# A graph layer's kernel: the order of the first loads, and the order of work behind the last gather

## The chip, the cores and the metric

The kernel runs on one core of a Trainium2 chip. A core has a matrix engine (TensorE, PE in the profile; PEld is its loading of weights), a vector engine (VectorE, DVE), a scalar engine (ScalarE, ACT), a general engine (GpSimd, POOL) and SyncE (SP), which here only issues transfers. SP and ACT have a hardware queue for transfers each; POOL issues gathers by indices through a queue that is written by software. All queues share 16 DMA engines. The metric is the time of one execution on the device, in microseconds; the time before is the median of three runs.

## The reference

A graph layer with 12,500 nodes of 96 channels and 412,500 edges, sorted by target node:

```
node_feat = mlp(x, W_node, ...)                   # relu, then normalized over all nodes
edge_feat = mlp(edge_attr_4, W_edge, ...)         # relu, then normalized over all edges
message   = mlp(concat(x[src], x[dst], edge_feat), W_msg, ...)   # relu, normalized over all edges
agg       = segment_sum(message, dst)
out       = layernorm(x + agg + node_feat)        # per node
```

Each `mlp` normalizes each channel with the mean and the variance over all its rows. The mean and mean square of the messages are therefore known only when the last edge has been worked on; scale and shift of the messages are applied behind the sum over edges.

## The kernel before, in words

*Tables.* x lies transposed in SBUF (`xp`, 96 partitions, 98 blocks of 128 nodes). `tables` (L153) multiplies each block by two thirds of W_msg and writes two tables to DRAM: `p_tab`, for the source node of an edge, and `q_tab`, for the target node. It goes by chunks of 14 blocks (`CH`), with two buffers of rows, and its writes alternate between the queues of SP and ACT.

*Gathers.* Edges go in tiles of 128, in groups of 4 tiles and blocks of 4 groups: 3,223 tiles, 806 groups, 202 blocks. For each tile POOL issues one gather (`gather`, L179) of the 128 source rows. The first 16 groups (`RAW` = 4 blocks, 64 gathers) are gathered from x itself, by a small piece of the indices (`src_raw`) that is loaded first of all, so that they need not wait for the tables; later (`convert`) TensorE multiplies them by the weights. All others come from `p_tab`, by `src`. The first 26 blocks (`SPILL`) are gathered while the statistics of nodes and edges are still being made, and written back to DRAM by SP; from then on gathers fill a ring of 26 groups (`RING`).

*Between.* `places`, `nodes` and `edge_norm` prepare the edges' places, the nodes' part and the edge statistics while the gathers go on.

*The main loop* (L624 to L663) works group by group in an order written out by hand for all five engines: `edges` and `prepare` compute the edge features, `linear` multiplies by weights and the window of `q_tab` rows, `message` (L514) adds the gathered rows. The message is clipped at zero and split into bf16 parts: `first_part` (L531, ACT), `second_part` (L566 on DVE, L567 on ACT), `third_part` (L572, DVE). `clipped` and `squared` (L537 and L541, ACT) make the squares for the statistic. `sums` (L584) multiplies by a 0/1 matrix, so that TensorE adds the edges of a node; `fold` (L590), `turn` (L594) and `add` (L607, L608) put a block's sums into `agg`.

*The end* (L665 to L708). The last block has two groups; `last` is the first of them, and `n - 1`, of three tiles, is the other. Each is worked on alone. POOL, which has no gathers left, adds up the squares (`collect`, L553 to L561). At the very end a product with a column of ones (L696) adds them over the partitions, and some small DVE and ACT instructions (L700 to L149) turn the sums into scale and shift. The stage `output` (L862) multiplies `shift` by a centering matrix (L868), then `agg` by a matrix `dm` (L879), and normalizes each node in 13 blocks.

*Unread products.* `unread` (L464) makes TensorE multiply 128x128 parts of `rel` by the identity, into a PSUM buffer that nobody reads: they keep the engine busy where it would have nothing to do. A call with n makes n products of 512 columns, two passes each.

The order of SP and POOL in the first part, and that of all engines in the main loop and the end, is that of the program's text; elsewhere a scheduler orders the instructions of an engine. Each engine executes its own in order, and so do the queues of transfers. What is in front of an instruction on its engine thus delays it.

Of the kernel before, what the change touches and what calls it, by code (L numbers as in the profile page):

```python
# [11 lines left out]
F32 = mybir.dt.float32  # L12
# [9 lines left out]
N, C, E, ED = 12500, 96, 412500, 4  # L22
EPS = 1e-5
P = 128
# [3 lines left out]
GT, GE, BG = 4, 512, 4  # L28
# [11 lines left out]
NB = -(-N // P)  # L40
NN = NB * P
NBK = 4
CH = 14
# [15 lines left out]
NW = WS * (BG - 1) + WN + 1  # L59
OW = NW * GT + WS * (BG - 1)  # L60
CL, CE = 2, 2
BUSY = 2
J = 8


# [12 lines left out]
def gnn(ctx, tc, t):  # L78
    nc = tc.nc
# [11 lines left out]
    src = const.tile([P, NTP], I32, name="src")  # L91
# [2 lines left out]
    ring = rpool.enter_context(tc.tile_pool(name="ring", bufs=RING // 2))  # L94
    xp = xpool.enter_context(tc.tile_pool(name="x", bufs=1)).tile([C, NN], F32, name="xp")
    nc.scalar.dma_start(w_msg, t["L0_gnn_W_msg"].rearrange("(s k) f -> k s f", k=C))
    for i in range(0, NB, CH):
        part = slice(i * P, (i + CH) * P)
        (nc.scalar if i // CH % 2 else nc.sync).dma_start(xp[:, part], t["xp"][:, part])
    nc.scalar.dma_start(src, t["src"])  # L100

    ident = const.tile([P, P], F32, name="ident")
    make_identity(nc, ident)
# [24 lines left out]
    rel = const.tile([P, NGP, GT], F32, name="rel")  # L128
# [224 lines left out]
    def fast(ring):  # L353
# [13 lines left out]
        with tc.manual_schedule(engines={ET.SP, ET.Pool}):  # L367
# [12 lines left out]
            n = 0  # L380
# [18 lines left out]
        with tc.tile_pool(name="fix", bufs=1) as fix, tc.tile_pool(name="msg", bufs=2) as work, \  # L399
# [62 lines left out]
                        got[b * BG + i] = back[:, i, :, :]  # L462

            def unread(n):  # L464
                busy = ps.tile([P, GE], F32, name="pa")
                for i in range(n):
                    nc.tensor.matmul(busy, ident, rel[:, i * P:(i + 1) * P, :].rearrange("p g t -> p (g t)"),
                                     start=True, stop=True)

            def convert(s):  # L470
# [62 lines left out]
            def clipped(k, m=2, n=GT):  # L533

                z, h = parts(k, m, n)
                sq = work.tile([P, 2, GT, C], F32, name="sq")
                nc.scalar.activation(sq[:, :m, :n, :], z, AF.Relu)  # L537
                return sq

            def squared(sq, m=2, n=GT):  # L540
                nc.scalar.activation(sq[:, :m, :n, :], sq[:, :m, :n, :], AF.Square)  # L541
                return sq, m, n
# [8 lines left out]
            def collect(x, n, r=P):  # L551

                plus = nc.gpsimd.tensor_add  # L553
                whole = n if r == P else n - 1
                if r < P:
                    plus(squares[:r], x[:r, whole * C:n * C], squares[:r])
                while whole > 1:
                    half = whole // 2
                    plus(x[:, :half * C], x[:, :half * C], x[:, (whole - half) * C:whole * C])
                    whole -= half  # L560
                plus(squares, x[:, :C], squares)  # L561

            def second_part(k, m=2, n=GT):

                z, h = parts(k, m, n)
                nc.vector.scalar_tensor_tensor(z, z, 0.0, h[0], op0=OP.max, op1=OP.subtract)  # L566
                nc.scalar.activation(h[1], z, AF.Copy)  # L567

            def third_part(k, m=2, n=GT):

                z, h = parts(k, m, n)
                nc.vector.tensor_tensor(h[2], z, h[1], op=OP.subtract)  # L572

            def sums(k):

                s, g = steps[k]
                n = min(GT, NT - g * GT)
                i = g % BG
                h, o = hb[s % HB][:, i, :, :, :], WS * (BG - 1 - i)
                if i == 0:  # L580
                    pas[s] = ps.tile([P, GE], F32, name="pa")
                for t in range(n):
                    r = min(P, E - (g * GT + t) * P)
                    nc.tensor.matmul(pas[s][:NW, :3 * (C + 1)], at[s % HB][:r, i, o + NW * t:o + NW * (t + 1)],  # L584
                                     h[:r, t, :, :].rearrange("p a c -> p (a c)"),
                                     start=i == 0 and t == 0, stop=t == n - 1 and (i == BG - 1 or g == NG - 1))
# [6 lines left out]
            def turn(s):  # L593
                nc.tensor.transpose(pas[s][:C + 1, GE - P:GE - P + NW], by_node.pop(s), ident[:NW, :NW])  # L594
# [16 lines left out]
            with tc.manual_schedule(engines={ET.SP, ET.Pool, ET.PE, ET.DVE, ET.Activation}):  # L611
                bad = nc.values_load(flag, min_val=0, max_val=1, skip_runtime_bounds_check_because="a comparison's result")
                load(0)
                fetch(0)
                load(1)
                fetch(1)
                for half in range(2):
                    edges(0, half)
                    prepare(0, half)
                edges(1, 0)  # L620
                for k in range(3):
                    linear(k)
                waiting, last = None, BG * (len(order) - 1)
                for k in range(last):  # L624
                    s, g = steps[k]
                    if g % BG == 0:
                        if s + 2 < len(order):
                            load(s + 2)
                            fetch(s + 2)
                    message(k)  # L630
                    j = k - LATER - BG - 1
                    if k % 2:
                        first_part(k - 1)
                        now = squared(clipped(k - 1))
                        if waiting:
                            moments(*waiting)
                        waiting = now
                        second_part(k - 1)
                    if j >= 0 and j % BG == 0:
                        fold(j // BG)  # L640
                    if j >= 2 and j % BG == 2:
                        add(j // BG, place(j // BG))
                    if k % 2:
                        third_part(k - 1)
                    if j >= 1 and j % BG == 1:
                        turn(j // BG)
                    if k >= LATER:
                        sums(k - LATER)
                    if g % BG != 3 and s + 1 < len(order):
                        if g % 2:  # L650
                            edges(s + 1, 1)
                        else:
                            prepare(s + 1, g % BG // 2)
                    if g % BG == 3:
                        if s + 1 < len(order) and order[s + 1] < RAW:
                            convert(s + 1)
                        if s + 2 < len(order):
                            edges(s + 2, 0)
                    if k + 3 < n:
                        linear(k + 3)  # L660
                    if g >= SPILL:
                        got[ahead] = ahead_of(ahead)
                        ahead += 1  # L663

                s, g = len(order) - 1, steps[last][1]  # L665
                m, r = NT - (g + 1) * GT, E - (NT - 1) * P
                collect(waiting[0].rearrange("p g t c -> p (g t c)"), 2 * GT)
                message(last)
                first_part(last, 1, GT)
                sq = clipped(last, 1, GT)  # L670
                turn(s - 2)
                add(s - 2, place(s - 2))
                sums(last - 2)
                sums(last - 1)
                unread(1)
                second_part(last, 1, GT)
                message(n - 1)
                first_part(n - 1, 1, m)
                squared(sq, 1, GT)
                collect(sq[:, 0, :, :].rearrange("p t c -> p (t c)"), GT)  # L680
                third_part(last, 1, GT)
                sums(last)
                fold(s - 1)
                at_end = place(s - 1), place(s)
                sq = clipped(n - 1, 1, m)
                second_part(n - 1, 1, m)
                turn(s - 1)
                squared(sq, 1, m)
                collect(sq[:, 0, :, :].rearrange("p t c -> p (t c)"), m, r)
                add(s - 1, at_end[0])  # L690
                third_part(n - 1, 1, m)
                sums(n - 1)
                square_sum = ps.tile([P, 2, GE], F32, name="pr", bufs=1)[:C, 0, :1]
                fold(s)
                turn(s)
                nc.tensor.matmul(square_sum, squares, ones, start=True, stop=True)  # L696
                unread(BUSY)
                mean_square = fix.tile([C, 1], F32, name="mean_square")
                add(s, at_end[1])
                nc.vector.tensor_scalar(mean_square, square_sum, 1.0 / E, None, op0=OP.mult)  # L700
                ahead_of(ahead)
                ahead_of(ahead + 1)
# [233 lines left out]
```

## Time and profile before

| | |
|---|---|
| time, median of 3 runs | 4107.81 us (4106.57 to 4109.8) |
| time of the profiled execution | 4088.25 us |
| its span | 4086.1 us |
| POOL busy | 3068.8 us, 75% of the span |
| PE, DVE, ACT busy | 3149.9, 2578.6, 2033.7 us |
| mean granted TensorE clock | 0.631 |
| moved by DMA | 274.06 MB, 67 GB/s in the mean |

How to read it: an engine's busy time is the sum of its instructions; between two gathers POOL also spends time on issue, which isn't counted as busy. The clock is a share of full speed, as granted to TensorE over a stretch. In a list of groups stands the line, the engine, the operation, what is written and read, how often, the total in us and the mean in ns, then the idle time ahead of them and what ended it. In the order of time a row has its start, its duration, engine, line, operation, and in brackets the idle time before it with what ended that. The chain is followed back from the last instruction, at each step to what released it.

### The profile page before, as it was taken

How to read it: one execution, taken by the hardware profiler on the slowest of the kernel's cores; microseconds unless marked ns; L12 is line 12 of the kernel's file. 1: busy time of each engine (PE TensorE's matmuls, PEld its weight loads, DVE VectorE, ACT ScalarE, POOL GpSimd, SP SyncE). 2: the span in 40 equal slices, each digit the busy share in tenths (PEclk: the TensorE clock that was granted, in tenths of full speed). 3: DMA queues.
4: the chain of work that ended last, by engine and by line, in shares of the span. 5: the costliest groups of instructions: out<-in, count | busy, mean ns of one | idle time of the engine just before them, and what ended most of it. 6: DMA issues, size and time to landing. Idle time of an engine off the chain costs nothing.

```text
span 4086.1 us, 42638 instructions
## 1 busy us (share of the span) xinstructions
PE 3149.9 (77%) x13544; PEld 2305.1 (56%) x13544; DVE 2578.6 (63%) x4036; ACT 2033.7 (50%) x2422; POOL 3068.8 (75%) x3252
## 2 busy tenths in 40 slices
PE   4699958888887777777777777777777777767876
PEld 3456636666665555555555555555555555555555
DVE  2599985666776655665566556655666556656666
ACT  1388845555555544454445444544444444544444
POOL 7777777777777777777777777777777777777776
PEclk7655556666666666666666666666666666666667
DMA  8555532222222122212212222122212221222123
GB/s 229 176 120 116 114 82 55 54 55 55 56 55 51 50 53 54 54 46 54 52 48 54 52 55 53 46 53 54 54 46 54 54 54 46 54 52 55 46 76 96
DMA packets 194110, 274.06 MB, mean 67 GB/s; under 512 B 121987, under 2 KB 122372, under 8 KB 192870
## 3 DMA queue, kind: packets, MB, share of 16 engines
q0 software_dynamic: 103136, 158.62, 16.3%
q1 hardware_dynamic: 77300, 103.96, 9.2%
q10 hardware_dynamic: 13440, 8.65, 0.8%
q8 instruction: 111, 1.82, 0.2%
q14 instruction: 123, 1.01, 0.1%
HBM read 227.56 MB, written 43.43 MB: 66 GB/s over the span
## 4 chain that ended last, share of the span: by engine, by line
POOL 46%; issue 18%; DMA 16%; PE 11%; DVE 8%; ACT 1%; DVEq 0%; POOLq 0%; ACTq 0%
POOL pg L179 46%; DMA pg<-p_tab,src 15%; PE z L505 5%; PE pa L584 3%; DVE sum_of L547 3%; PE pr L491 2%; DVE z L514 1%; DVE z L566 1%; ACT h L567 1%; DVE h L572 1%; DVE at L518 1%; PE pr L480 1%; DVE squares L549 0%; DMA pg<-in_x,src_raw 0%; PE pr L476 0%
## 5 line engine op out<-in xcount | busy, mean ns | idle before, releaser
L179 POOL DMA_INDIRECT pg<-p_tab,src x3159 | 2986.3, 945 | 966.1 <-issue 857.5
L505 PEld LDWEIGHTS z<-rhs,left 128*128 128x128 f32 x6446 | 1301.2, 297 | 1003.0 <-DVE h L572 887.9
L505 PE MATMUL z<-rhs,left 128*128 128x96 f32 x6446 | 1389.3, 388 | 566.7 <-DVE h L572 562.7
L531 ACT ACTIVATE h<-z 128x768 bf16<-128x768 f32 x404 | 329.9, 817 | 1352.3 <-DVE z L514 1346.9
L584 PE MATMUL pa<-h,at 128*80 128x291 bf16 x3223 | 850.4, 411 | 185.7 <-DVE at L518 181.8
L514 DVE TENSOR_TENSOR z<-z,pg 128x384 f32<-128x384 f32 x702 | 395.1, 563 | 773.1 <-DMA pg<-p_tab,src 741.2
L584 PEld LDWEIGHTS <-at 128*80 128x80 bf16 x3223 | 499.3, 168 | 299.2 <-DVE at L518 226.0
L547 DVE TENSOR_REDUCE sum_of<-sq 128x96 f32<-128x768 f32 x401 | 589.3, 1469 | 0.0
L499 ACT ACTIVATE left<-pr 127x1024 f32<-127x1024 f32 x403 | 410.8, 1019 | 307.2 <-PE pr L491 306.7
L572 DVE TENSOR_TENSOR h<-z,h 128x768 bf16<-128x768 f32 x404 | 386.8, 957 | 243.3 <-ACT h L567 242.8
L491 PE MATMUL pr<-ea,we 7*127 7x512 f32 x1404 | 498.8, 793 | 17.8 <-DMA ea<-rel_d 12.6
L566 DVE SCALAR_TENSOR_TENSOR z<-z,h 128x768 f32<-128x768 f32 x404 | 387.3, 959 | 30.4 <-ACT sq L537 30.2
L316 PE MATMUL pr<-ea,wide 10*128 10x512 f32 x1212 | 359.6, 1084 | 8.2 <-DMA ea<-in_ea 8.2
L322 DVE BATCH_NORM_STATS2 estats<-r 128x6 f32<-128x512 f32 x606 | 359.9, 676 | 7.8 <-ACT r L320 7.8
L567 ACT ACTIVATE h<-z 128x768 bf16<-128x768 f32 x404 | 328.9, 814 | 66.9 <-DVE z L566 66.9
L320 ACT ACTIVATE r<-pr 128x1024 f32<-128x1024 f32 x303 | 306.6, 1023 | 106.3 <-PE pr L316 62.8
L541 ACT ACTIVATE sq<-sq 128x768 f32<-128x768 f32 x404 | 339.7, 841 | 12.8
L537 ACT ACTIVATE sq<-z 128x768 f32<-128x768 f32 x404 | 323.2, 800 | 0.3 <-DVE h L572 0.3
L316 PEld LDWEIGHTS pr<-ea,wide 10*128 10x128 f32 x1212 | 239.6, 309 | 126.9 <-issue 65.7
L518 DVE TENSOR_TENSOR at<-rel,z 128x496 bf16<-128x496 f32 x202 | 135.6, 671 | 252.5 <-PE z L505 252.5
L491 PEld LDWEIGHTS pr<-ea,we 7*127 7x127 f32 x1404 | 133.3, 233 | 145.3 <-issue 127.0
L549 DVE TENSOR_TENSOR squares<-sum_of,squares 128x96 f32<-128x96 f32 x401 | 104.4, 260 | 13.8
(127 smaller groups left out, 1071.4 us busy)
## 6 DMA issues: line engine op xcount, KB each, us to landing
pg<-p_tab,src POOLq DMA_INDIRECT x3159
spill<-pg SPq DMA_DIRECT2D x52, 384.0 KB
pb<-spill SPq DMA_DIRECT2D x26, 768.0 KB
ea<-in_ea SPq DMA_DIRECT2D x75, 160.0 KB
rhs<-q_tab SPq DMA_DIRECT2D x202, 46.5 KB
ea<-in_ea SPq DMA_DIRECT2D x352, 20.0 KB
y_d<-y0s SPq DMA_DIRECT2D x12, 384.0 KB
pg<-y_d SPq DMA_DIRECT2D x12, 384.0 KB
```

Source lines behind the costliest of these rows:

```text
L179: nc.gpsimd.indirect_dma_start(out=pg[:, i, :], out_offset=None, in_=tab[:, :], in_offset=bass.IndirectOffsetOnAxis(ap=idx[:, k:k + 1], ax ...
L316: nc.tensor.matmul(pr[:, k % 2, :], wide[Q * i:Q * i + 2 * EK, :], ea[Q * i:Q * i + 2 * EK, b % J, :], start=True, stop=True)
L322: nc.vector.bn_stats(stats[:, (k - o) % NS, (k - o) // NS, :], r[:, 1 - o, :])
L491: nc.tensor.matmul(prs[s, half][:C + WN, i, :], we[o:o + EK + 2, :], block[s][o:o + EK + 2, :], start=True, stop=True)
L499: nc.scalar.activation(x[:C + WN, 2 * half:2 * half + n, :], pr[:C + WN, :n, :], AF.Relu)
L505: nc.tensor.matmul(zb[k // 2 % 2][:, k % 2, i * C:(i + 1) * C], left[s % 2][:KR, g % BG, i * P:(i + 1) * P], rhs[:KR, s % RB, g % BG, :], ...
L514: nc.vector.tensor_add(z, z, got.pop(g)[:, :n, :])
L547: nc.vector.tensor_reduce(sum_of, sq[:, :m, :n, :].rearrange("p g t c -> p c g t"), axis=AX.XY, op=OP.add)
L566: nc.vector.scalar_tensor_tensor(z, z, 0.0, h[0], op0=OP.max, op1=OP.subtract)
L567: nc.scalar.activation(h[1], z, AF.Copy)
L572: nc.vector.tensor_tensor(h[2], z, h[1], op=OP.subtract)
L584: nc.tensor.matmul(pas[s][:NW, :3 * (C + 1)], at[s % HB][:r, i, o + NW * t:o + NW * (t + 1)], h[:r, t, :, :].rearrange("p a c -> p (a c)") ...
```

## The change

At the start, x is loaded by SP alone, in 14 transfers of 7 blocks, where SP and ACT took turns in 7 transfers of 14 blocks; the sources (`src`, 1,616 KB) follow on SP's queue where they followed on ACT's.

At the end, for the last group: `clipped` now precedes the squaring of the group before it, and `second_part` precedes the collection of those squares, the sums of `last` and the fold of block s - 1; `third_part` precedes the addition of block s - 1. The sum of squares is written to a free column of the last block's own PSUM buffer. The unread products have 256 columns and are written to the buffer of the edges' products. There are four in the place of the first one, one ahead of `turn(s - 1)`, one behind `sums(n - 1)`, and five where two were at the end.

```
-BUSY = 2
+BUSY = 5
...
-    for i in range(0, NB, CH):
-        part = slice(i * P, (i + CH) * P)
-        (nc.scalar if i // CH % 2 else nc.sync).dma_start(xp[:, part], t["xp"][:, part])
-    nc.scalar.dma_start(src, t["src"])
+    for i in range(0, NB, CH // 2):
+        part = slice(i * P, min(i + CH // 2, NB) * P)
+        nc.sync.dma_start(xp[:, part], t["xp"][:, part])
+    nc.sync.dma_start(src, t["src"])
...
             def unread(n):
-                busy = ps.tile([P, GE], F32, name="pa")
+                busy = ps.tile([P, 2, GE], F32, name="pr", bufs=1)[:, 0, :GE // 2]
                 for i in range(n):
-                    nc.tensor.matmul(busy, ident, rel[:, i * P:(i + 1) * P, :].rearrange("p g t -> p (g t)"),
+                    nc.tensor.matmul(busy, ident, rel[:, i * P:i * P + P // 2, :].rearrange("p g t -> p (g t)"),
                                      start=True, stop=True)
...
                 first_part(last, 1, GT)
-                sq = clipped(last, 1, GT)
+                sq = [clipped(last, 1, GT)]
                 turn(s - 2)
                 add(s - 2, place(s - 2))
                 sums(last - 2)
                 sums(last - 1)
-                unread(1)
+                unread(BUSY - 1)
                 second_part(last, 1, GT)
                 message(n - 1)
                 first_part(n - 1, 1, m)
-                squared(sq, 1, GT)
-                collect(sq[:, 0, :, :].rearrange("p t c -> p (t c)"), GT)
+                sq.append(clipped(n - 1, 1, m))
+                squared(sq[0], 1, GT)
                 third_part(last, 1, GT)
+                second_part(n - 1, 1, m)
+                collect(sq[0][:, 0, :, :].rearrange("p t c -> p (t c)"), GT)
                 sums(last)
                 fold(s - 1)
                 at_end = place(s - 1), place(s)
-                sq = clipped(n - 1, 1, m)
-                second_part(n - 1, 1, m)
+                unread(1)
                 turn(s - 1)
-                squared(sq, 1, m)
-                collect(sq[:, 0, :, :].rearrange("p t c -> p (t c)"), m, r)
+                squared(sq[1], 1, m)
+                collect(sq[1][:, 0, :, :].rearrange("p t c -> p (t c)"), m, r)
+                third_part(n - 1, 1, m)
                 add(s - 1, at_end[0])
-                third_part(n - 1, 1, m)
                 sums(n - 1)
-                square_sum = ps.tile([P, 2, GE], F32, name="pr", bufs=1)[:C, 0, :1]
+                unread(1)
                 fold(s)
                 turn(s)
+                square_sum = pas[s][:C, GE - P + NW:GE - P + NW + 1]
                 nc.tensor.matmul(square_sum, squares, ones, start=True, stop=True)
                 unread(BUSY)
```

## The prediction, made before the result was known

> **What bounds the kernel now.** I read the page's busy times and its chain, then who waited for whom on GpSimd (POOL), then the order of time at both ends, since the change touches nothing between them.
>
> ```profile
> span 4086.1 us, 42638 instructions
> POOL 46%; issue 18%; DMA 16%; PE 11%; DVE 8%; ACT 1%; DVEq 0%; POOLq 0%; ACTq 0%
> L179 POOL DMA_INDIRECT pg<-p_tab,src x3159 | 2986.3, 945 | 966.1 <-issue 857.5
> ```
>
> ```profile
> POOL pg L179 <- issue: 874.3, 2868, 0.5
> POOL pg L179 <- DMA pg<-p_tab,src: 85.4, 270, 1.6
> POOL pg L179 <- DMA pg<-in_x,src_raw: 6.1, 8, 1.6
> ```
>
> POOL issues 3,223 gathers, 3,159 from p_tab and 64 from x. One takes 0.945 us and 874.3/2868 = 0.305 us of issue follows: 1.25 us each, 4,029 us in all of a span of 4,086.1. Its chain agrees: gathers on POOL, their issue and the landings. So POOL is the bound from the first gather to the last. A microsecond elsewhere counts only if it keeps POOL waiting, or if it lies behind the last gather. The waits of POOL for landings have 0.30 us of ordinary issue in each: 6.1 - 8 x 0.30 = 3.7 us are lost at the x gathers, 85.4 - 270 x 0.30 = 4.4 us at the others.
>
> The longest of these waits, 1.64 us, and the first p_tab gather, in order of time:
>
> ```profile
> 24.96 0.94 POOL L179 DMA_INDIRECT pg<-in_x,src_raw  x1 [1.64 <-DMA pg<-in_x,src_raw]
> ...
> 85.62 3.53 DVE L228 TENSOR_TENSOR rel<-dsti,basei 128x3232 f32<-128x3232 int32 x1 [18.73 <-DMA basei<-in_base]
> 86.77 3.19 POOL L179 DMA_INDIRECT pg<-p_tab,src  x1 [0.30 <-issue]
> ```
>
> And two pieces of the chain, start, us and what, one while x is loaded and one from the main loop:
>
> ```profile
> 14.52 13.31 DMA pg<-in_x,src_raw
> 654.66 2.40 DMA pg<-p_tab,src
> ```
>
> A gather that lands after 2.40 us in the main loop takes 13.31 us while x and the sources come in on SP's and ACT's queues. At 1.25 us per gather that is ten behind, and POOL then waits for old ones to land.
>
> **The change at the start.** It takes three x transfers and the sources from ACT's queue and gives SP 14 transfers of 96 x 896 numbers (336 KB) and then the sources (128 x 3232 numbers, 1,616 KB), 6.3 MB together, as before. Stretches of the start, with the DMA share and GB/s in the last columns, and a wait of SP's queue (total, times, longest):
>
> ```profile
> 2.00:8.00 6.00, 0.00 (x0) 0.00 (x0) 0.24 (x2) 1.28 (x1) 3.95 (x4) 1.00 1.02 275
> 17.00:28.00 11.00, 7.44 (x45) 6.80 (x43) 1.91 (x2) 0.81 (x1) 5.65 (x6) 0.94 1.01 293
> 31.00:78.00 47.00, 23.24 (x116) 22.14 (x116) 9.30 (x10) 6.67 (x11) 35.45 (x38) 0.72 1.00 263
> 80.00:85.00 5.00, 0.00 (x0) 0.00 (x0) 0.00 (x0) 0.00 (x0) 3.78 (x5) 0.50 0.88 351
> SPq L224 <- DMA q_tab<-trow: 5.7, 1, 5.7
> ```
>
> With both queues loading, the engines move 275 to 293 GB/s at a share of 1.0. From 80 to 85 us SP alone loads a 1,616 KB tensor with gathers beside it: 351 GB/s, and POOL issues its five gathers in 5 us, without a stall. That row is nearest to the new start: one hardware queue, long rows, gathers beside it. So I take the whole 3.7 us as gained. The ends: nothing gained, if any full load delays gathers as two do; and 3.7 + (3.19 - 0.94) = 5.9 us, if the slow first p_tab gather goes too. I do not count that one: it runs beside the long VectorE subtraction of L228, which the change leaves.
>
> The Trainium skill, "DMA: Bandwidth & Descriptors", section "Queues, rings and completion order", says that each DMA engine takes its queue rows in turn, a packet at a time. By that a gather beside two loading rows waits for two long packets per turn and beside one for one, and of half the length; the trace's 13.31 against 2.40 us agrees, and the sum by it would be the same.
>
> SP's queue is now passed by ten more x issues and the sources. Their issue is covered by the transfers (four issues took 2.23 us, row below, so 14 take some 8 us against over 20 us of data). Queued behind them on SP are the small loads of L209 to L220 and the first table writes. The tables are the one thing POOL needs from there. SP's load of dst, at 78.03 us, waits for the last q_tab write, so the tables are in DRAM by 78 us at the latest, and with POOL 3.7 us earlier the first p_tab gather is due at 83.1: 5 us of cover. From 31 to 78 us the DMA engines are full with table writes, so what is loaded sooner or later moves that end about one for one. At 351 instead of 290 GB/s it would move forward. I cost the move at nothing; without cover each microsecond costs one. ACT, rid of four issues, is not on the path. Ahead of the main loop nothing else feeds POOL.
>
> ```profile
> 1.27 2.23 SPq L99 DMA_DIRECT2D xp<-in_xp  x4
> 78.03 0.34 SPq L224 DMA_DIRECT2D dsti<-in_dst  x1
> ```
>
> **The change at the end.** The chain behind the last gather, then rows beside it from the order of time, then stretches of the end with the clock, the DMA share and GB/s last (in the text 41.57 stands for 4041.57, and so on):
>
> ```profile
> 4037.95 2.69 DMA pg<-p_tab,src
> 4040.76 0.48 DVE z L514
> 4041.26 0.42 ACT h L531
> 4041.70 0.57 DVE h L572
> 4042.36 0.42 ACT sq L537
> 4042.80 0.48 DVE z L566
> 4043.30 0.42 ACT h L567
> 4043.75 0.47 DVE h L572
> 4044.26 0.90 PE pa L584 x3
> 4045.18 0.47 DVE by_node L590
> 4046.34 3.62 PE pa L467 x4
> 4049.97 0.34 PE pd L868 x2
> 4050.64 4.00 PE py L879 x32
> ```
>
> ```profile
> 4038.71 1.91 PE L467 MATMUL pa<-rel,ident 128*128 128x512 f32 x2
> 4041.57 0.51 ACT L541 ACTIVATE sq<-sq 128x384 f32<-128x384 f32 x1
> 4042.32 0.70 PE L584 MATMUL pa<-h,at 128*80 128x291 bf16 x4 [1.69 <-DVE h L572]
> 4042.86 0.23 PE L594 MATMUL pa<-ident,by_node 80*97 80x80 f32 x1
> 4048.25 0.15 DVE L149 TENSOR_TENSOR shift<-vec,norm_win 96x1 f32<-96x1 f32 x1
> ```
>
> ```profile
> 4042.00:4046.00 4.00, 1.96 (x10) 1.26 (x11) 2.25 (x7) 1.23 (x4) 2.47 (x6) 0.78 0.08 25
> 4046.00:4050.00 4.00, 4.00 (x9) 1.88 (x8) 1.58 (x11) 0.29 (x1) 0.00 (x0) 0.50 0.01 2
> 4054.00:4080.00 26.00, 18.95 (x170) 18.78 (x169) 23.31 (x39) 14.27 (x26) 15.99 (x11) 0.90 0.63 163
> ```
>
> (1) The second clipping moves ahead of the squaring of L541 on ACT: it can start at 41.57 instead of 42.36. Its subtraction on VectorE still stands behind the L572 that ends at 42.27, so L566 begins there instead of at 42.80: 0.5 us gained. The fold of the block before (0.47 us by the L590 row) now runs on VectorE beside ACT's L567 of 0.42, and the last L572 keeps the gain.
>
> (2) Unread products. They now write the bank of the edges' products, whose last reader, the last block's preparation, comes before the last messages; I count no wait for it. One of full width, two passes, took 1.91 us at half clock; one of half width then takes 0.95, and 0.48 at full clock. Four in the place of one run from 4038.71 to about 4042.5 at half clock, against 4042.32, where the next product waits for its data: up to 0.2 us, and that product has a microsecond to spare. The new one ahead of the turn of s - 1 stands in front of the last sums: 43.0 + 0.48 + 0.23 for a turn is 43.7, some 0.4 later at half clock, and the data now come at about 43.25 (43.75 less the 0.5): the half microsecond of (1) is lost again, all of it and up to 0.4 more. The one behind the last sums is covered by the fold of 0.47, if the clock is full; at half clock it delays the turn by 0.5.
>
> (3) The sum of squares moves to a free column of the block's own bank. It waits for POOL's collection as before; I take nothing.
>
> (4) Five of half width stand where two of full width took 3.62 us of the chain, in front of L868, whose data (L149) are ready at 48.40, while it starts at 49.97. At half clock five take 4.8 us, 1.1 more; at full clock 2.4. All full: the products end before the data, so L868 starts when these are there, at 48.40 or a little before (say 48.2), 1.8 us sooner, and the first 32 output products take 32 x 18.95/170 = 3.6 instead of 4.0 us: 2.2 us gained. All half: 1.1 lost here, 0.5 in the turn, and up to 0.4 ahead of the last sums, of which none is covered: 2.0 us lost. Which it is, rows can't say: the clock was 0.78 from 4042 to 4046 with PE busy 1.96 of 4 us, then 0.50. With PE now busier by about a microsecond there, I take full clock from a quarter of the five on: 1.2 + 1.8 = 3.0 us instead of 3.62, L868 0.6 us sooner, and the 0.4 behind it, 1.0 us in all.
>
> The Trainium skill, "TensorE: Matmul & The Clock Gate", Part 1, says the clock is half until a window of some 3.4 us was busy. By that rule, where the added products fill the window before the five, the end would gain the 2.2 us of the first case, and the time by it is 4107.81 - 3.7 - 2.2 = 4101.9; the trace's 0.50 behind a stretch with PE half idle agrees with it.
>
> Behind L868 the output stage is unchanged, 13 blocks of VectorE work.
>
> **The sum.** 3.7 + 1.0 = 4.7 us of the profiled execution's 4088.25, which lies 19.6 us under the median of the runs, 4107.81. No row shows where these 19.6 us are, so I take the difference over: 4107.81 - 4.7 = 4103.1. What the likeliest case may be by its own terms: 4107.81 - 5.9 - 2.2 = 4099.7 to 4107.81 - 3.7 + 2.0 = 4106.1. A measurement of this kernel tells about 0.2% from no change, 8.2 us: this gain stays inside it.
>
> **Rivals.** *The stall stays.* Gathers queue behind any full load, whatever the number of queues. For it: the first stalls come after 14 us, when loads had been running for long. Against it: the row from 80 to 85 us. The time is then 4107.81 - 1.0 = 4106.8.
>
> *More goes than the profile has.* The runs take 19.6 us more than the profiled execution; if a part of that is gathers queueing behind the loads, then the change removes it too. For it: landings are the only thing POOL waits for that isn't fixed issue. Against it: no row. With the 4.4 us of the later landing waits as a size, the gain is 4.7 + 4.4 = 9.1 us: 4098.7; its far end is 4.7 + 19.6 = 24.3.
>
> *The tables come late* (the other side). Were SP's short transfers not overlapped, each would cost its landing, 2.40, and 0.344 MB at 351 GB/s, 1.0: 14 x 3.4 us, with the sources' 2.4 + 4.7 us 54.7 us of loading, where it now takes some 27 (to about 28 us in the stretches above). The tables would come 28 us later, and POOL would wait 28 - 5 = 23 us of them: 23 - 4.7 = 18.3 us slower, 4126.1. It decides from 9.7 us of delay on (no gain left) and from 17.9 on is slower by over 0.2%. Against it: SP issued four transfers in 2.23 us without waiting for one, and the row at 351 GB/s. The same page on DMA, of the Trainium skill, section "Rules for kernel authors", speaks for it: it wants 1 MiB and more per transfer. With its 2.0 us of fixed cost per transfer and 436 GB/s, unoverlapped, the loads would take 14 x 2.8 + 5.8 = 45 us, an estimate from that page; no run here shows it.
>
> **Chances.** The forecast 0.56, the stall stays 0.12, more goes 0.20, late tables 0.12. Faster by over 0.2%: all of "more goes" and 0.04 of the forecast's far end (with a microsecond for what the rows can't show), 0.24; slower: late tables, 0.12; within: 0.64. The range 4097 to 4109 takes in the forecast's own, the stall that stays and half of "more goes", and leaves out the rest with the late tables.
>
> **What would show it.** The wait of the x gathers for landings is gone and the first p_tab gather starts near 83 us; if it starts there later than 86.8, the tables are late. The x gathers land in a few us. At the end L537 of the last group precedes L541, the clock from 4042 to 4050 (less 3.7) is above 0.6, and from the last L514 to L868 it takes some 8 us; it takes 49.97 - 40.76 = 9.21 now. Wrong it is if POOL's issue itself changes (1.25 us per gather), for 0.003 us of that is 10 us of the time.

## The result, and the profile after

The changed kernel takes 4082.57 us in the median (4081.86 to 4084.07, six runs) against 4106.3 for the kernel before (4105.54 to 4109.8, six runs): the ratio is 0.9941, with a 95% interval from 0.9928 to 0.9954, 23.7 us less. The gain is larger than forecast, and the time lies below the forecast, 4103.1, and below its range, 4097 to 4109.

One thing has to be known to read any number here: executions of the kernel before lie at two levels, some near 4089 us and some near 4106, with nothing between. The six runs above are all at the upper one; the execution whose profile was shown, 4088.25 us, is at the lower. All of the changed kernel's executions are at one level. The two profiled executions therefore compare a lower level with a lower level, and differ by 5.9 us only (4088.25 and 4082.31). Five of the runs below were on chips where every kernel, the one before too, took some 5,500 to 5,600 us, with stretches in which TensorE, VectorE and ScalarE stand idle while POOL issues on; of these only the traces are used.

The page of the changed kernel, in its span, its chain and its gathers, and then POOL's waits:

```profile
span 4080.0 us, 42678 instructions
POOL 48%; issue 21%; PE 13%; DMA 9%; DVE 8%; ACT 2%; DVEq 0%; POOLq 0%; ACTq 0%
L179 POOL DMA_INDIRECT pg<-p_tab,src x3159 | 2983.9, 945 | 965.5 <-issue 899.0
```

```profile
POOL pg L179 <- issue: 918.2, 3010, 1.1
POOL pg L179 <- DMA pg<-p_tab,src: 41.5, 130, 1.5
```

The row for landings of x gathers is gone: POOL no longer waits while x is loaded, and the x gathers land after 6.0 us in the median (3.8 to 8.0). The gathers' own pace is as before. In the order of time, in the waits of SP's queue, and in a stretch of the loading:

```profile
72.84 0.45 SPq L224 DMA_DIRECT2D dsti<-in_dst  x1
...
81.31 3.52 DVE L228 TENSOR_TENSOR rel<-dsti,basei 128x3232 f32<-128x3232 int32 x1 [18.64 <-DMA q_tab<-zero]
81.87 3.78 POOL L179 DMA_INDIRECT pg<-in_x,src_raw  x1 [0.30 <-issue]
85.95 0.94 POOL L179 DMA_INDIRECT pg<-p_tab,src  x1 [0.30 <-issue]
```

```profile
SPq L99 <- DMA xp<-in_xp: 10.7, 6, 4.2
SPq L100 <- DMA q_tab<-trow: 10.7, 1, 10.7
```

```profile
17.00:28.00 11.00, 4.26 (x27) 3.97 (x25) 0.06 (x1) 0.24 (x1) 8.45 (x9) 0.78 1.08 278
```

The load of dst, which waits for the last table write, is issued at 72.84 instead of 78.03: the tables are there 5 us sooner, by 72.84 at the latest. The gather that is held up beside the long VectorE subtraction of L228 is now the last one from x, with 3.78 us instead of 3.19. The loading itself is not faster on one queue: 256, 241 and 278 GB/s from 2 to 8, 8 to 17 and 17 to 28 us, where before had 275, 257 and 293. The fourteen issues of x take 16.80 us on SP, not the some 8 forecast, since six of them wait for earlier x loads, 10.7 us in all. The sources wait 10.7 us for a table write, a wait that the prediction did not see; nothing needs them before the first p_tab gather.

The end, in the chain, then the last z addition from the order of time, and two stretches with the clock (third number from the right):

```profile
4034.03 0.94 POOL pg L179
...
4037.64 0.42 ACT sq L537
4038.08 0.57 DVE h L572
4038.68 0.48 DVE z L566
4039.18 0.42 ACT h L567
4039.62 0.47 DVE h L572
4040.14 0.55 PE pa L584 x3
...
4041.71 2.27 PE pr L467 x10
4044.10 0.40 PE pd L870 x2
...
4044.84 3.83 PE py L881 x32
```

```profile
4036.82 0.47 DVE L514 TENSOR_TENSOR z<-z,pg 128x288 f32<-128x288 f32 x1 [1.37 <-DMA pg<-p_tab,src]
```

```profile
4038.00:4042.00 4.00, 2.95 (x17) 2.23 (x18) 2.79 (x9) 1.20 (x4) 2.47 (x6) 1.00 0.10 27
4042.00:4046.00 4.00, 3.51 (x22) 2.79 (x21) 1.59 (x11) 0.29 (x1) 0.00 (x0) 1.00 0.01 2
```

The clock is full from 4038 on, where it was 0.78 and then 0.50 in the stretches shown of before. The last unread products take 2.27 us of the chain instead of 3.62. From the last gather's issue to the centering product it now takes 44.10 - 34.03 = 10.07 us, and 49.97 - 37.95 = 12.02 before: 1.95 us less.

### The profile page after: what moved, and what is told of

The parts are those of the page before. It is cut to its first block, busy times and chain, and to the rows that moved or that the text cites. A ratio compares the mean times of both kernels' runs of the same rounds, so it can differ in the third digit from the quotient of the medians.

```text
span 4080.0 us, 42678 instructions
## 1 busy us (share of the span) xinstructions
PE 3168.7 (78%) x13560; PEld 2327.9 (57%) x13560; DVE 2576.6 (63%) x4036; ACT 2036.5 (50%) x2422; POOL 3069.2 (75%) x3252
## 4 chain that ended last, share of the span: by engine, by line
POOL 48%; issue 21%; PE 13%; DMA 9%; DVE 8%; ACT 2%; DVEq 0%; POOLq 0%; ACTq 0%
POOL pg L179 48%; DMA pg<-p_tab,src 9%; PE z L505 6%; PE pa L584 3%; DVE sum_of L547 2%; PE pr L491 2%; DVE z L514 1%; DVE z L566 1%; ACT h L567 1%; DVE h L572 1%; DVE at L518 1%; PE pr L480 1%; DVE squares L549 0%; PE pr L476 0%; ACT xt L478 0%
## 5 line engine op out<-in xcount | busy, mean ns | idle before, releaser
L514 DVE TENSOR_TENSOR z<-z,pg 128x384 f32<-128x384 f32 x702 | 395.0, 563 | 764.1 <-DMA pg<-p_tab,src 733.3
L572 DVE TENSOR_TENSOR h<-z,h 128x768 bf16<-128x768 f32 x404 | 386.9, 958 | 244.2 <-ACT h L567 243.2
L491 PE MATMUL pr<-ea,we 7*127 7x512 f32 x1404 | 514.6, 817 | 17.8 <-DMA ea<-rel_d 12.6
L566 DVE SCALAR_TENSOR_TENSOR z<-z,h 128x768 f32<-128x768 f32 x404 | 387.3, 959 | 35.6 <-ACT sq L537 35.5
L316 PEld LDWEIGHTS pr<-ea,wide 10*128 10x128 f32 x1212 | 251.0, 310 | 115.2 <-issue 57.9
```

Source lines behind the costliest of these rows:

```text
L316: nc.tensor.matmul(pr[:, k % 2, :], wide[Q * i:Q * i + 2 * EK, :], ea[Q * i:Q * i + 2 * EK, b % J, :], start=True, stop=True)
L491: nc.tensor.matmul(prs[s, half][:C + WN, i, :], we[o:o + EK + 2, :], block[s][o:o + EK + 2, :], start=True, stop=True)
L514: nc.vector.tensor_add(z, z, got.pop(g)[:, :n, :])
```

## The experiments

Wherever times are given below, the kernel before has its two levels on the same chip. Levels are told apart at 4096.5 us.

**The kernel before, unaltered.**

> The kernel before, unaltered, run as a kernel of its own. The changed kernel's timed executions are 23.7 us faster than those of before (4082.57 against 4106.3), while the two profiled executions differ by 5.9 us only (4082.31 against 4088.25). Theory A (both times of before are its own, some executions have a loss of some 18 us that others lack): executions scatter over 4088 and 4106, or the profiled one shows 4106 and where the 18 us are. Theory B (the profile of before came from a better chip or day): timed and profiled both near 4106, or both near 4088, and the real effect is either 24 or 6 us.

Measured: 4089.3 to 4091.3 in 5 executions and 4105.3 to 4107.7 in 7; its comparison on the same chip, again the kernel before, has 19 executions with a median of 4089.55 and 16 with 4105.83. So theory A holds: one program, one chip, two levels 16.3 us apart. The profiled execution of this run was a lower one, so it did not show where they part.

**The start alone, the end alone, and both.** `start_only` has the part of the diff that loads x and the sources, `end_only` all the rest.

```
...
-        (nc.scalar if i // CH % 2 else nc.sync).dma_start(xp[:, part], t["xp"][:, part])
-    nc.scalar.dma_start(src, t["src"])
...
+        nc.sync.dma_start(xp[:, part], t["xp"][:, part])      # 14 parts of CH // 2 blocks
+    nc.sync.dma_start(src, t["src"])
```

> x and the sources on SP's queue alone, the end as before. By the two profiles (last gather 3.9 us earlier) it is 3.9 us faster than before, some 4084.3 against a profile of 4088.25. If the 18 us that only timed executions of before have are gathers held up behind the two queues' loads, it is 22 us faster in timed executions. If they have to do with the end, 4 us faster.

> The new end, the loads as before. By the two profiles (2.2 us less behind the last gather) it is 2.2 us faster. If the 18 us have to do with the end or with the mere shift of the program, it is 20 us faster; if with the loads, 2 us, near 4104.

> The changed kernel beside the others on one chip: 4082.6, or 23.7 us under before, if the chip is not what makes the difference; 6 us under before if before shows 4088 here.

Measured, 12 executions each, beside before's 4089.55 and 4105.83:

| | lower level, executions, median us | upper level, executions, median us |
|---|---|---|
| start_only | 6, 4083.71 | 6, 4101.86 |
| end_only | 12, 4086.89 | none |
| both_again | 12, 4083.28 | none |

The ratios to before, levels mixed, are 0.999 (0.9972 to 1.0009), 0.9976 (0.9962 to 0.999) and 0.996 (0.9947 to 0.9973). The start doesn't touch the levels: half and half, as in before. The new end has only the lower one. So the 16.3 us hang on the end, and the theory of gathers held up by the loads falls. What each part gives within the lower level depends on the pair that is compared: the start 4086.89 - 4083.28 = 3.6 us beside the new end, but 4089.55 - 4083.71 = 5.8 beside the old one; the end 2.7 us (4089.55 - 4086.89) beside the old start, but 0.4 (4083.71 - 4083.28) beside the new one. Together they give 6.3 us either way; the medians fix the split to some 2 us only. The traces fix the end: from the last gather's issue to the end of the span it takes 47.6 to 48.2 us in `before`, `same` and `start_only`, and 46.0 to 46.1 in the three with the new end. That is some 1.9 us, which leaves some 4.4 for the start. POOL's waits agree on where the start's gain is. `end_only` still has the row for landings of x gathers:

```profile
POOL pg L179 <- DMA pg<-in_x,src_raw: 7.3, 9, 1.5
```

In `start_only` that row is gone, and only the one for the gathers from p_tab is left:

```profile
POOL pg L179 <- DMA pg<-p_tab,src: 84.5, 275, 0.6
```

**No products at the very end.** The new theory is that TensorE's clock makes the levels: full in the output stage or half, and the unread products ahead of it decide.

```
                 nc.tensor.matmul(square_sum, squares, ones, start=True, stop=True)
-                unread(BUSY)
```

> The kernel before, without its two unread products at the very end. Before takes 4088 to 4091 us in some executions and 4104 to 4108 in the others, and the new end has only the lower. Clock theory: in the upper ones TensorE's clock is at half when the output stage begins and stays there, so that its 196 passes take some 0.2 us instead of 0.11, 17 us in all, and the products ahead of it decide. Then this kernel is in the upper state in all or nearly all executions, near 4104 (before's 4106 less 1.6, since the centering product no longer waits), its output stage shows a clock of 0.5 and is bound by PE. Rival (the upper state comes from elsewhere, a transfer or the main loop): both states as often as before, each some 1.6 us lower, and the clock in the output stage is high.

> The kernel before without its last unread products, again: the first time every kernel took 5,550 to 5,600 us with pauses of all engines, and only the traces could be read. There its output stage had a busy PE for 42.1 us, 422 ns a pass, where kernels with products had 22.1 us and 275 ns. Clock theory: all executions near 4104 to 4106, none near 4089. Rival (half clock in the output stage doesn't cost the 17 us): both of before's levels.

The second run gave times: 12 of 12 at the upper level, median 4106.2 (before beside it 4090.13 in 19 and 4107.56 in 16). The profiled execution, of 4107.28 us, is at last one of the upper level: its output products, who waited for them, and two stretches of its output stage (the three durations of a row are the shortest, the median and the longest, in ns):

```profile
L878 PE MATMUL py<-dm,agg x196: 421/421/529, 4052.8 to 4094.5; 97*128 97x96 f32 x196
```

```profile
  DVE y L884: 19.6, 12
```

```profile
4056.00:4060.00 4.00, 4.00 (x21) 4.00 (x20) 0.96 (x1) 0.84 (x1) 0.00 (x0) 0.50 0.00 0
...
4064.00:4068.00 4.00, 4.00 (x21) 4.00 (x20) 3.44 (x7) 1.55 (x4) 2.96 (x3) 0.50 0.21 55
```

PE is busy without a gap at a clock of 0.50, and VectorE waits for it 19.6 us. In the profile of before, at the lower level, the same 196 passes show (first their durations and VectorE's wait, then a stretch of that stage, then a stage near the start with the stretch around it):

```profile
L879 PE MATMUL py<-dm,agg x196: 275/275/529, 4050.6 to 4072.7; 97*128 97x96 f32 x196
...
  DVE y L885: 3.1, 2
```

```profile
4060.00:4064.00 4.00, 4.00 (x38) 4.00 (x38) 3.89 (x7) 2.77 (x4) 3.11 (x3) 1.00 0.88 229
```

```profile
L288 PE MATMUL py<-center,xp x196: 421/421/528, 140.6 to 195.9; 96*128 96x96 f32 x196
```

```profile
138.00:197.00 59.00, 42.76 (x196) 42.04 (x196) 36.02 (x25) 13.37 (x10) 44.98 (x47) 0.50 0.45 149
```

421 ns a pass against 275 (passes overlap): the stage takes 41.7 us on PE (4052.8 to 4094.5) where it took 22.1 (4050.6 to 4072.7). VectorE's wait for it grows by 19.6 - 3.1 = 16.5 us, which is the 16.3 us between the levels. At full clock VectorE's work is the longer one (3.89 of 4.00 us) and hides PE; at half clock PE is the bound. L288 is another stage, with the same kind of products, and the clock was 0.50 from its start to its end in the profile shown of before. It could have been read there.

All other traces fit. The eight of lower executions have 275 ns in the output stage, the three of upper ones 421 ns (`after_no_last` from its first passes on); of the five with no level, `five_half`, `four_full` and `four_full_2` have 275, `no_end_products` and `order_bare` 421. No upper execution of the kernel before itself was profiled: that its upper level is the same clock is concluded from this kernel, which lies at that level and differs by the two products at the end alone.

**Which products decide.** Three kernels: before with five halves at the end instead of two whole ones (and two halves for the first whole one), and the changed kernel without its five last products or with these alone.

```
 five_half:                                      # on before
-                busy = ps.tile([P, GE], F32, name="pa")
+                busy = ps.tile([P, GE], F32, name="pa")[:, :GE // 2]
...
-                    nc.tensor.matmul(busy, ident, rel[:, i * P:(i + 1) * P, :].rearrange("p g t -> p (g t)"),
+                    nc.tensor.matmul(busy, ident, rel[:, i * P:i * P + P // 2, :].rearrange("p g t -> p (g t)"),
...
-                unread(1)
+                unread(2)
...
-                unread(BUSY)
+                unread(5)
 after_no_last:                                  # on the changed kernel
-                unread(BUSY)
 after_only_last:
-                unread(BUSY - 1)
-                unread(1)                       # both
```

> The kernel before with five unread products of half width at the end (4.3 us at half clock in the place of 3.4), the first unread product as two halves, all else as before. Clock theory, if the length of the last burst alone decides: the upper state becomes rarer than before's half of the executions, yet does not vanish, since the burst is only 0.9 us longer: 1 to 4 of 12. If the products ahead of it, between the sums, are what the new end lives by, upper in about half of them. The lower state 4089 to 4091.

> The kernel before with five half products at the end, again. If the length of the last burst alone decides: 1 to 4 of 12 executions at the upper level near 4106, the others near 4089.5. If the products ahead of it decide: about half at the upper level, as before.

> The changed kernel without the five last products; the four first ones and the two between the sums stay. If the clock that these raise lasts until the output stage, all executions are near 4083, as with the five. If the five are needed, since PE idles from the sum of squares to the centering product, some 3 us, part of the executions or all are near 4099 to 4101.

> The changed kernel with the five last products alone, the six ahead of them gone. If the early ones are what makes the clock certain: part of the executions, a quarter to a half, near 4100, the others 4083 to 4085. If the five suffice: all at 4083 to 4085.

| | lower level, executions, median us | upper level, executions, median us |
|---|---|---|
| five_half_2 | 10, 4091.01 | 2, 4107.94 |
| after_no_last | none | 12, 4100.94 |
| after_only_last | 9, 4087.16 | 3, 4103.37 |

The five are needed: without them PE idles for 2.40 us ahead of the centering product, and the clock, raised before, is lost. Two rows of `after_no_last`, the output products and the first stretch behind its centering product (at 4043.03):

```profile
L880 PE MATMUL py<-dm,agg x196: 275/421/422, 4043.8 to 4085.0; 97*128 97x96 f32 x196
```

```profile
4044.00:4048.00 4.00, 4.00 (x22) 4.00 (x22) 0.95 (x1) 0.00 (x0) 0.00 (x0) 0.54 0.00 0
```

The first passes still have 275 ns, all later ones 421. And the five alone do not suffice in every execution. The profiled one of `after_only_last` (4103.26 us) is of the upper level; its chain:

```profile
4043.64 4.47 PE pr L467 x10
4048.11 0.34 PE pd L867 x2
...
4048.79 41.29 PE py L878 x192
4090.10 0.97 DVE y L884
```

The five take 4.47 us, all at half clock, and then 41.29 us of the chain are PE alone. In `five_half_2` they took less, the clock rose among them, and the stage was at full clock:

```profile
4047.06 3.90 PE pa L467 x10
4050.96 0.18 PE pd L868 x2
4051.48 3.83 PE py L879 x32
```

**The changed kernel without any unread product** (the four calls of `unread` removed) has a trace only.

> The changed kernel without any unread product: its loads, its order of work at the end. Clock theory: upper state in nearly all executions, near 4100 (start_only's upper 4101.8 less 1.6). If instead the order of work removes the upper state, all executions lie near 4082 to 4084, and the products are for nothing.

The trace has the stage at half clock:

```profile
L877 PE MATMUL py<-dm,agg 97*128 97x96 f32 x196 | 42.1, 422 | 0.4 <-DVE dm L869 0.4
```

So in this execution the new order without products did not raise the clock; how often it would is open.

**A longer burst, with nothing early.**

```
-                unread(BUSY)
+                unread(2 * BUSY)                # on before: four of full width
```

> The kernel before with four unread products of full width at the end in the place of two. Clock theory: 6.8 us of unbroken products at half clock hold a whole window of the clock's control wherever it falls, so the upper state is gone: all executions near 4089, up to 3.4 us above or 1 below, as the products themselves delay the centering product (at half clock by 3.4, less where the clock rises among them). Rival: both states as before, each up to 3.4 us later.

> The kernel before with four products of full width at the end in the place of two, again (the first time on a chip that paused). Two gave about half of the executions the lower level, five of half width about four in five, none gave none. If the clock rises after a window of some 3.4 us that was busy throughout, wherever the window falls, an unbroken 6.8 us always holds one: 12 of 12 at the lower level, 4089 to 4092. If the early products of the new end are needed to make it certain, some executions stay near 4106 to 4110.

> As for four_full_2, which also fell on a chip where every kernel took over 5,500 us: 12 of 12 at the lower level, 4089 to 4092, if an unbroken busy stretch that holds a whole window is what counts; some near 4106 to 4110 if the early products are needed.

The third run has times: 12 of 12 at the lower level, 4089.8 to 4092.8, median 4091.48; before beside it 8 executions at 4088.2 to 4090.2 and 8 at 4104.4 to 4109.4. So the early products are not needed for all executions to reach full clock, as far as twelve show it; a long enough burst does it. But it costs: its eight passes are 5.78 us of the chain, and the median is 2 us above before's lower level.

```profile
4049.20 5.78 PE pa L467 x8
4054.98 0.18 PE pd L868 x2
4055.51 3.83 PE py L879 x32
```

Put together, by the length of the last burst at half clock: nothing, 0 of 24 executions at the lower level; two whole products (3.62 us in the prediction's row), before in all these comparisons, 51 of 104 (the result's six, all upper, among them); five halves (4.47), 19 of 24; four whole (twice 3.62), 12 of 12. And with the six early halves ahead of the five, 30 of 30 (end_only, both_again and the result's six).

The Trainium skill, "TensorE: Matmul & The Clock Gate", Part 1, says that the clock rises after a busy window of some 3.4 us, and that the windows run freely, so that a program meets them at any phase. By that rule the share of executions with a whole window in the burst grows by 0.85/3.4, a quarter, for each 0.85 us more, and is certain from twice a window on. The trend agrees: from two whole products to five halves the burst grows by 4.47 - 3.62 = 0.85 us and the share by 0.79 - 0.49 = 0.30 (give or take 0.2), and four whole ones give 12 of 12. The shares themselves don't come out: for the burst alone the rule would give (3.62 - 3.4)/3.4 = 0.06 and (4.47 - 3.4)/3.4 = 0.31.

The burst is thus not all that counts. In the profile of before the clock still is 0.50 when the burst ends, at 4049.97; it rises only near 4051.0, behind the centering product, in the first passes of the output stage (0.62 in the mean of these four us, so a quarter of them at full clock):

```profile
4048.00:4052.00 4.00, 3.64 (x15) 2.27 (x14) 0.66 (x4) 0.00 (x0) 0.00 (x0) 0.62 0.00 0
```

Which of the products around the burst count with it is open. That windows are what decides is argued from the counts, and no run moved a window. Shown is that the products at the end decide the level, and that a longer burst makes the lower one more frequent.

## Why the prediction was right or wrong

- *POOL is the bound between the ends; its pace doesn't change.* Right: 945 ns a gather in both profiles.
- *Two queues delay the x gathers, one does not; 3.7 us gained.* Right that the wait goes, and near in size: the start gave 3.6 or 5.8 us by the medians, some 4.4 by the traces. *The stall stays* fell with it. That it is the number of queues is not shown: in the same edit the transfers became half as long, and SP held some of them back until earlier ones had landed. The row from 80 to 85 us, 351 GB/s, was no guide to the rate (241 to 278 GB/s). In the traces of other kernels with the old loads the x gathers lose more than in the one shown: in `end_only` 7.3 - 9 x 0.30 = 4.6 us.
- *The tables move at no cost, with 5 us of cover.* Right in effect, but not as argued: the prediction let the first table writes queue behind the loads on SP, and ACT be of no account. In fact the first write went out on ACT's queue during the load of x, at 12.72 us (below) where it was 30.57 before. TensorE had begun the tables at 5.32 instead of 8.82, as the first, shorter x load had landed; the sources were what waited, and the tables came 5 us sooner. *The tables come late* fell. The 45 us that the prediction put beside it, worked out from figures of the Trainium skill, "DMA: Bandwidth & Descriptors", section "Anatomy of one DMA — SWDGE (gpsimd) path", use a fit that the page gives for transfers issued from GpSimd; these loads are issued from SP.

```profile
12.72 0.41 ACTq L172 DMA_DIRECT2D q_tab<-trow  x1
```

- *The slow first p_tab gather stays.* Right: 2.8 us are still lost beside L228 (3.78 - 0.94), at the gather ahead of it. So it hangs on the subtraction and not on the first p_tab gather, which starts at 85.95 us, later than the 83 that was named as the sign.
- *(1), the earlier clipping, 0.5 us.* Right in kind, too large: from the start of the last L514 (36.82, before 40.76) the last L566 begins after 1.86 us instead of 2.04, and the last L572 after 2.80 instead of 2.99: 0.2 us, since the L572 of the group before, behind which L566 stands, now itself begins 0.3 us later (1.26 us after L514 instead of 0.94, when the clipping moved ahead is done).
- *(2) and (3), the other products and the sum of squares.* At full clock the early ones cost what was allowed and no more: the last sums start 3.32 us after L514 (40.14 - 36.82) instead of 3.50.
- *(4), the centering product 0.6 us sooner by a clock that rises among the five.* Undersized: the clock was full ahead of the five, the case priced with 2.2 us. Behind the last gather the end now takes some 1.9 us less in the traces, and from the last L514 to the centering product 44.10 - 36.82 = 7.28 us instead of 9.21 (some 8 were forecast).
- **The step that failed** is the sum's sentence that no row shows where the 19.6 us between the profiled execution and the runs are, "so I take the difference over". They were the upper level, and it is made in the very stretch that the change works on. Behind it stands a mis-sized term of (4): of the clock in the output stage only the first 32 products were priced, 0.4 us, as though the stage would get its full clock by itself a moment later. It does not: at half clock it stays there for all its 41 us, and the stage is then bound by PE, 16.3 us longer. A row in the profile of before could have warned of it: L288, 196 such passes at 421 ns, against L879 at 275.
- *More goes than the profile has* was right in that the change takes the difference (its far end, 24.3 us, is near the 23.7 measured), and wrong in its place: the gathers at the start gave only some 4.4 us of it.

In levels: 16.3 (no more upper level) + 6.3 (start and end within the lower level) = 22.6 us, against the 23.7 of the medians. That all six runs of before behind these medians were upper ones is luck, or the chip's doing: in the other comparisons 51 of 98 were lower. With a lower median of before, the measured gain would have been near 6.3 us, not far from the 4.7 forecast, and the levels would not have shown. Where half of before's executions are lower ones, as in three of the comparisons, the same change is worth less: 0.996 on the chip of `both_again`.

## What to carry to other kernels

When a profiled execution and the timed runs differ by more than the runs scatter among themselves, the difference is not a constant to take over: look at every single time for levels, and look for a stage whose bound depends on a state, such as TensorE's clock, before predicting. A stage of short products behind an idle TensorE may never reach full clock by itself; a burst of wide unread products ahead of it decides for the whole stage, and its length decides in what share of the executions. Gathers that share the DMA engines with loads can be held up by the way the loads are issued: with x on SP alone, in transfers of half the length, POOL's wait was gone, though the loads moved no faster. Which of the two did it, the queues or the length, would need a run of its own.

## What the runs showed of the hardware that was not expected

A busy TensorE doesn't raise its clock whatever it does: in the upper level's output stage it is busy 4.00 of 4.00 us in stretch after stretch for 41 us, with passes of 96 columns that each have their own weights, and the clock stays at 0.50. Around bursts of 256 or 512 columns it rose in every lower execution that was profiled, at the latest some 5 us behind the burst's start (before, 4046.21 to near 4051.0), though not in the one of `after_only_last`, after 4.47 us of them. The page on TensorE of the Trainium skill that is named above would have it rise after one busy window; here the measurement decides. Why these passes don't raise the clock isn't shown. They do keep it: where a burst ran right up to the stage at full clock, as in the changed kernel, the stage kept it to the end of its passes; in `after_no_last`, where PE had idled ahead of it, it was lost after the first passes.
